# Layer 0's weights moved to the free axis by VectorE transpositions, and paired Strassen products in another order

## The chip, the cores and the metric

The kernel runs on one core of a Trainium2 chip. The metric is the device time of one execution in microseconds (us), taken as the median of repeated runs. A profile of one such execution gives the time of every instruction on the five engines: TensorE (PE, its weight loads PEld), VectorE (DVE), ScalarE (ACT), GpSimd (POOL) and the queue of SyncE (SP), which issues the DMA transfers here.

## The reference

A stack of four graph layers works on 128 graphs of 64 nodes with 512 features, all in float32. Before every layer there is a layer norm and a ReLU, after it the layer's output is added to x. The layer that the first half of the change touches is layer 0:

```python
h = jnp.maximum(_layernorm(x), 0.0)              # (128, 64, 512)
q, k = jnp.split(h @ Wqk, 2, axis=-1)
v = h @ Wv
agg = jnp.einsum('bij,bjd->bid', adj, k * mask[:, :, None])
w = inv_scale * mask * jnp.einsum('bid,bid->bi', q, agg)      # one number per node
x = x + jax.nn.softmax(w, axis=1)[:, :, None] * v             # over the 64 nodes of a graph
```

So each graph has 64 numbers w, one for each node, and a softmax over them. Layer 1 is an attention over the 64 nodes with adj as a factor (`weight = adj * exp(query @ key.T)`, divided by its row sums, times value). Layer 2 is an eight-headed attention with an output projection. Layer 3 mixes three powers of a transition matrix, each with its own weight.

## The kernel before, in words

**Tiles.** The 8192 nodes ("tokens") are cut into 32 blocks of 256 tokens, that is two halves of 128 (`TT = 2`). A half has one token on each of the 128 partitions, so a partition range of 64 is one graph. The normalised block `h` is transposed by TensorE (`transposed`, line 191) to `hT`, and copied out of PSUM by ACT (line 194) for one half and DVE (line 196) for the other.

**The products.** Every multiplication of a 256x512 block by a 512x512 weight is done by seven products of half size (the Winograd form of Strassen's method). The sums of quarters of the weight are formed once (`formed`); the sums of quarters of the block are formed by POOL for each block (`sums`, lines 215 to 218): S1 = A21 + A22, S2 = S1 - A11, S4 = A12 - S2, S3 = A11 - A21. Product 1 needs only `hT`, product 5 needs S1, product 6 needs S2 and product 4 needs only `hT`. A `Product` owns two PSUM banks, `ab` (quarters a and b) and `dc` (quarters d and c). Products 1 and 6 write `ab`, products 5 and 4 write `dc`; these four are the early ones. Then `keep_ab` copies a to `p1` (ACT, line 275) and makes `u2 = b + p1` (DVE, line 276), and `keep_dc` copies c to `p5` (ACT, line 283 or 287). Only then may the late products 2, 7 and 3 add to the same banks. The outputs are put together by `store` or `store_T` (DVE lines 298 to 314, ACT lines 297 and 318, POOL lines 301 and 321).

In the trace the early and the late products of one kind carry the same name: `ab_g`, `dc_g` are those of the first weight of a step ("g"), `ab_v`, `dc_v` those of the second ("v"); `ab_q` and `ab_k` are layer 2's.

**Two products side by side.** `side_by_side` takes one or two parts that share the block. It writes, in program order: `first` of part 1 (products 1 and 6, `keep_ab`), then the work listed in `between[0]`, then `second` of part 1 (products 5 and 4, `keep_dc`), both of part 2, then the late products of part 1 with the work of `between[1]` ahead of them, the late products of part 2 with `between[2]` ahead. Layers 0 and 1 and the q and k of layer 2 go through it with two parts; the output projection of layer 2 with one; layer 3 has its own order.

**Steps.** Layers 0 and 1 run in steps of one block: layer 0 of blocks b and b+1, then layer 1 of b and b+1, and so on through the 32 blocks, so that four steps make a round. The end of a layer-0 step, `layer0_end`, is put off into `between[0]` of the step behind it. There also stands `prepare`, the norm of the block of the step after that (DVE lines 168 to 175, POOL line 173, ACT line 180), and in `between[2]` its transposition. So in the second and the third step of a round DVE and ACT have the put-off softmax of layer 0 and the norm that layer 1 needs from its result.

**Layer 0's softmax.** In `layer0`, w comes out as one number per partition (line 504, a product with a running sum, for each half). The softmax needs all 64 numbers of a graph on the free axis. Line 511 (DVE) spreads w by the identity to `wd` (128 x 2 x 64, a diagonal for each half). In `layer0_end` `graph_sums` (line 392, TensorE) multiplies it by `ones_bd`, which has ones in the blocks of a graph: each partition then has the 64 numbers of its graph in PSUM, named `sm_w` in the trace. Line 522 (DVE) takes the minimum, line 525 subtracts, line 528 (ACT, once for each half) takes the exponential and its sum, line 533 (ACT) the exponential of the own number, lines 535 and 536 (DVE) make the weight, and line 538 (DVE) adds it times v to x.

**Order.** The source gives only data dependencies and a priority by program order. When the program is built, a scheduler writes one fixed list of instructions for each engine from that; on the chip each engine takes its list strictly in order and waits at the head of it.

Of the kernel before, what the change touches and what calls it, by code (L numbers as in the profile page):

```python
# [8 lines left out]
FP = mybir.dt.float32  # L9
AF = mybir.ActivationFunctionType  # L10
ALU = mybir.AluOpType
AX = mybir.AxisListType

P = 128
N = 64
# [3 lines left out]
TT = 2  # L19
# [6 lines left out]
def kernel(ctx: ExitStack, tc: tile.TileContext, a: dict, out: bass.AP):  # L26
# [7 lines left out]
    nc = tc.nc  # L34
# [9 lines left out]
    small = ctx.enter_context(tc.tile_pool(name="small", bufs=3))  # L44
# [8 lines left out]
    def rows(b: int):  # L53
        return slice(b * T, (b + 1) * T)

    def load_x(b: int, source, stage: int):
        x = big.tile([P, TT, D], FP, tag="x", name=f"x{stage}_{b}", bufs=4)
        nc.sync.dma_start(x, tokens(source))
        return x

    def load_adjT(b: int, stage: int):
        adjT = med.tile([P, TT, N], FP, tag="adjT", name=f"adjT{stage}_{b}")
        nc.sync.dma_start(adjT, tokens(adjT_d[rows(b), :]))
        return adjT
# [59 lines left out]
    first = load_x(0, x_d[rows(0), :], 0), load_adjT(0, 0)  # L124
# [16 lines left out]
    eye = const.tile([P, N], FP, tag="eye", name="eye")  # L141
    for g in range(2):
        h = slice(g * N, (g + 1) * N)
# [8 lines left out]
    for i in range(n_bd):  # L152
        e = const.tile([P, TT, P], FP, tag=f"bd{i}", name=f"bd{i}")
# [68 lines left out]
    class Product:  # L222
# [37 lines left out]
        def temp(self, tag):  # L260
            return snap.tile([P, F], FP, tag=tag, name=f"{tag}_{self.name}")

        def first(self, ops, w):
            self.early(ops, w, (1, 6))
            self.keep_ab()

        def second(self, ops, w, bias=None):
            self.early(ops, w, (5, 4))
            self.keep_dc(bias)

        def keep_ab(self):
# [23 lines left out]
        def store(self, y):  # L295

            nc.scalar.copy(y[:, 0, :F], self.a)
            nc.vector.tensor_tensor(self.u3, self.b, self.p1, ALU.add)  # L298
            nc.vector.tensor_tensor(y[:, 1, :F], self.d, self.u3, ALU.add)
            nc.vector.tensor_tensor(y[:, 0, F:], self.c, self.u2, ALU.add)  # L300
            nc.gpsimd.tensor_tensor(y[:, 1, F:], self.u3, self.p5, ALU.add)  # L301
# [37 lines left out]
    def side_by_side(*parts, between=()):  # L339

        between = iter(between)
        made = []
        for ops, w, bias, store, name in parts:
            p = Product(name, bias is not None)
            p.first(ops, w)
            if not made:
                for act in next(between, ()):
                    act()  # L350
            p.second(ops, w, bias)
            made.append(p)
        for p, (ops, w, bias, store, name) in zip(made, parts):
            for act in next(between, ()):
                act()
            p.late(ops, w)
            store(p)
        for acts in between:
            for act in acts:
                act()  # L360
# [16 lines left out]
    def neighbour_sums(ps, e, us):  # L377

        for t in range(TT):
            for g in range(2):
                nc.tensor.matmul(
                    ps[t][half[g ^ t]], e[half[g], t, :], us[t][half[g]], start=True, stop=True
                )
        return [(0, slice(0, P), slice(0, P))] + [(1, half[g], half[1 - g]) for g in range(2)]

    def graph_sums(e, cols: int, name: str):

        ps = ps_sc.tile([P, cols], FP, tag="sc", name=f"sm_{name}")
        nc.tensor.matmul(ps, ones_bd, e, start=True, stop=True)
        return ps
# [83 lines left out]
    def layer0_values(b: int, hT):  # L477
        ops = sums(hT, f"0_{b}")
        gv = big.tile([P, 2, TT, D], FP, tag="qk", name=f"gv_{b}")
        return ops, gv, (ops, w0v, None, lambda p: p.store(gv[:, 1]), f"v0_{b}")  # L480

    def layer0(b: int, x, adjT, hs, hT, between, ready=None):

        ops, gv, *part = ready or layer0_values(b, hT)
        am = small.tile([P, TT, N], FP, tag="am", name=f"am_{b}", bufs=2)
        nc.gpsimd.tensor_tensor(
            am,
            adjT,
            mcol[:, b * TT : (b + 1) * TT].unsqueeze(2).to_broadcast([P, TT, N]),
            ALU.mult,  # L490
        )
        pa = [ps_tr.tile([P, D], FP, tag="tr", name=f"pa_{b}_{t}") for t in range(TT)]
        aggs = [
            med.tile([P, D], FP, tag="agg", name=f"agg_{b}_{t}", bufs=2) for t in range(TT)
        ]
        for t, to, at in neighbour_sums(pa, am, hs):
            nc.scalar.copy(aggs[t][to], pa[t][at])

        side_by_side(
            (ops, m0, None, lambda p: p.store(gv[:, 0]), f"g0_{b}"), *part, between=between  # L500
        )
        w = small.tile([P, TT], FP, tag="w", name=f"w_{b}")
        for t in range(TT):
            nc.vector.scalar_tensor_tensor(
                aggs[t], gv[:, 0, t, :], msc[:, b * TT + t : b * TT + t + 1], aggs[t],
                ALU.mult, ALU.mult, accum_out=w[:, t : t + 1],
            )


        wd = small.tile([P, TT, N], FP, tag="e", name=f"wd_{b}")  # L510
        nc.vector.tensor_tensor(
            wd,
            eye.unsqueeze(1).to_broadcast([P, TT, N]),
            w.unsqueeze(2).to_broadcast([P, TT, N]),
            ALU.mult,
        )
        return x, gv, w, wd

    def layer0_end(b: int, x, gv, w, wd):
        wrow = graph_sums(wd.rearrange("p t i -> p (t i)"), TT * N, f"w_{b}")  # L520
        mn = small.tile([P, TT], FP, tag="mx0", name=f"mn0_{b}")
        nc.vector.tensor_reduce(
            mn, wrow.rearrange("p (t i) -> p t i", t=TT), AX.X, ALU.min
        )
        nc.vector.tensor_tensor(w, w, mn, ALU.subtract)
        tot = small.tile([P, TT], FP, tag="tot", name=f"tot_{b}")
        for t in range(TT):
            nc.scalar.activation(
                wd[:, t, :], wrow[:, t * N : (t + 1) * N], AF.Exp, bias=mn[:, t : t + 1],
                scale=-1.0, accum_out=tot[:, t : t + 1],  # L530
            )
        ex = small.tile([P, TT], FP, tag="ex", name=f"ex_{b}")
        nc.scalar.activation(ex, w, AF.Exp, scale=-1.0)
        att = small.tile([P, TT], FP, tag="att", name=f"att_{b}")
        nc.vector.reciprocal(att, tot)
        nc.vector.tensor_tensor(att, att, ex, ALU.mult)
        for t in range(TT):
            nc.vector.scalar_tensor_tensor(
                x[:, t, :], gv[:, 1, t, :], att[:, t : t + 1], x[:, t, :], ALU.mult, ALU.add
            )  # L540
# [75 lines left out]
    def layer2_in(b: int, hT, between=()):  # L616

        ops = sums(hT, f"2_{b}")
        qk = big.tile([P, 2, K, T], FP, tag="qk", name=f"qk_{b}")
        side_by_side(*(  # L620
            (ops, w, bias, lambda p, i=i, bias=bias: p.store_T(qk[:, i], bias), f"{'qk'[i]}2_{b}")
            for i, (w, bias) in enumerate(zip(made1[5], (b2q, b2k)))
        ), between=between)
        return qk, ops
# [318 lines left out]
    for i, (layer, b) in enumerate(steps):  # L943
        between = [[], [], []]
        for n, end in open_end:
            between[n].append(end)
        if i + 1 < len(steps):
            between[0].append(lambda: prepare(i + 1))
            between[2].append(lambda: turned(i + 1))
        else:  # L950
            between[0].append(lambda: prepare2(0))
            between[2].append(lambda: turned2(0))
        if layer == 0:
            softmax = layer0(b, *loaded[b], *normed[i], between, ready)
            ready = None
            open_end = [(0, lambda b=b, softmax=softmax: layer0_end(b, *softmax))]
        else:
            attention = layer1(b, *loaded[b], *normed[i], between)
            open_end = [
                (1, lambda b=b, a=attention: layer1_end(b, loaded[b][0], *a, x1[b]))  # L960
            ]
        if i == len(steps) - 3:
            setup = setup2()
            made2 = next(setup)
# [15 lines left out]
    qk, ops = layer2_in(0, normed2[0], [[], [end for _, end in open_end]])  # L980
# [6 lines left out]
    for b in range(n_blk):  # L987
        x, adjq = loaded2[b]
# [7 lines left out]
        if b + 1 < n_blk:  # L996
            qk, ops = layer2_in(b + 1, normed2[b + 1])
# [90 lines left out]
```

## Time and profile before

| | |
|---|---|
| median of 3 runs | 2751.52 us (2751.24 to 2751.78) |
| the profiled execution | 2750.76 us, span in the profile 2749.0 us |
| granted TensorE clock | 0.996 of full |
| PE busy | 2696.7 us, 98% of the span |
| DVE, POOL, ACT busy | 1628.3, 1279.6, 895.0 us |
| layers 0 and 1 | from the start to about 1060 us |
| one round of four steps | about 61.7 us (from one line 511 to the next but one) |

A line of the page or of a query gives the start and the duration in us, the engine, the source line, the operation, the tile written and the tile read, and in brackets how long the engine stood idle before it and what released it. A busy PE does not mean a PE at its peak, so what a stage costs is read from the starts of its instructions, not from busy time. The chain of waits follows the last instruction of a window back to what released it.

### The profile page before, as it was taken

Reading aid. Unit: us, or ns where it says so; the run is one execution under the profiler, and the core shown is the slowest. Engines: PE = TensorE matmul, PEld = TensorE weight load, DVE = VectorE, ACT = ScalarE, POOL = GpSimd, SP = SyncE. Lnnn points to the kernel's source line nnn. Section 1 sums busy time; section 2 is a strip of 40 time slices with the busy share of each in tenths; the row PEclk is TensorE's granted clock in tenths of the full one; section 3 lists DMA queues with packets and bytes.
Section 4 is the critical chain, followed back from the end, with each engine's and each line's share of the span. In section 5 each row is a group of like instructions: output and inputs, shape, how many; then the busy total and the mean of one; then the engine's idle time right before and its main releaser. Section 6 shows DMA issues by size and latency. Waiting matters only on the chain.

```text
span 2749.0 us, 53245 instructions
## 1 busy us (share of the span) xinstructions
PE 2696.7 (98%) x21336; PEld 2352.7 (86%) x21336; DVE 1628.3 (59%) x4105; ACT 895.0 (33%) x2132; POOL 1279.6 (47%) x1648
## 2 busy tenths in 40 slices
PE   7899999999999999999999999999989999999999
PEld 5688888888888887899999999999878888888888
DVE  4466666666656667565655655556546555565553
ACT  2233333333333333333333333333322222222221
POOL 2433434343333436555555555554455444444443
PEclk9999999999999999999999999999999999999999
DMA  4111101001111113111111111111111111111110
GB/s 143 40 42 34 49 33 34 34 34 34 44 39 41 41 34 102 38 36 36 53 36 43 46 36 53 36 36 53 48 49 58 57 50 50 50 50 50 50 49 31
DMA packets 102488, 128.53 MB, mean 47 GB/s; under 512 B 40544, under 2 KB 50016, under 8 KB 102240
## 3 DMA queue, kind: packets, MB, share of 16 engines
q1 hardware_dynamic: 100576, 123.02, 13.3%
q8 instruction: 168, 2.75, 0.4%
q10 hardware_dynamic: 1664, 2.10, 0.2%
q14 instruction: 80, 0.66, 0.1%
HBM read 74.76 MB, written 50.33 MB: 46 GB/s over the span
## 4 chain that ended last, share of the span: by engine, by line
PE 87%; DVE 6%; POOL 3%; ACT 2%; DMA 1%; issue 1%; SPq 0%; DVEq 0%; ACTq 0%; POOLq 0%
PE ab_y L250 12%; PE ab_v L250 10%; PE dc_y L250 9%; PE dc_v L250 7%; PE ab_q L243 4%; PE ab_k L243 4%; PE tr L191 4%; PE ab_o L250 4%; PE ab_g L250 4%; PE dc_k L243 3%; PE dc_q L243 3%; PE dc_o L250 3%; PE ab_g L243 3%; PE dc_g L250 2%; PE pz L849 2%; PE dc_g L243 2%
## 5 line engine op out<-in xcount | busy, mean ns | idle before, releaser
L180 ACT ACTIVATE h<-x,nmr,rstd 128x512 f32<-128x512 f32 x256 | 196.5, 807 | 197.8 <-DVE nmr L175 197.6
L173 POOL TENSOR_TENSOR rstd<-ve,neghalf 128x2 f32<-128x2 f32 x128 | 89.4, 699 | 351.3 <-DVE ve L171 351.2
L250 PE MATMUL ab_v<-L_Wv,hT 128*128 128x256 f32 x768 | 200.6, 384 | 2.3 <-DVE u_v L276 1.3
L250 PE MATMUL ab_v<-L_Wv,S 128*128 128x256 f32 x768 | 198.5, 381 | 0.8 <-POOL S L216 0.8
L250 PE MATMUL dc_v<-L_Wv,S 128*128 128x256 f32 x768 | 197.6, 380 | 0.0
L250 PE MATMUL ab_y<-L_Wk,S 128*128 128x256 f32 x768 | 187.3, 380 | 0.0
L168 DVE BATCH_NORM_STATS2 stats<-x 128x6 f32<-128x512 f32 x256 | 165.4, 679 | 27.3 <-DMA x<-x 22.0
L250 PE MATMUL dc_y<-L_Wk,S 128*128 128x256 f32 x768 | 177.9, 381 | 0.0
L194 ACT COPY hT<-tr 128x512 f32<-128x512 f32 x128 | 74.7, 584 | 304.3 <-PE tr L191 280.2
L215 POOL TENSOR_TENSOR S<-hT 128x256 f32<-128x256 f32 x128 | 108.2, 845 | 130.5 <-ACT hT L194 125.0
L250 PEld LDWEIGHTS ab_v<-L_Wv,S 128*128 128x128 f32 x768 | 147.0, 192 | 21.8 <-POOL S L216 1.6
L250 PEld LDWEIGHTS ab_y<-L_Wk,S 128*128 128x128 f32 x768 | 146.5, 191 | 20.1
L250 PEld LDWEIGHTS dc_v<-L_Wv,S 128*128 128x128 f32 x768 | 146.4, 191 | 20.1
L250 PEld LDWEIGHTS dc_y<-L_Wk,S 128*128 128x128 f32 x768 | 143.6, 190 | 18.2
L191 PE MATMUL tr<-ident,h 128*128 128x128 f32 x1024 | 142.5, 280 | 15.5 <-ACT h L180 13.2
L196 DVE COPY hT<-tr 128x512 f32<-128x512 f32 x128 | 87.5, 684 | 110.6 <-PE ab_v L250 106.7
L250 PEld LDWEIGHTS ab_v<-L_Wv,hT 128*128 128x128 f32 x768 | 135.1, 193 | 16.5 <-DVE u_v L276 1.7
L678 POOL TENSOR_TENSOR e<-e,r 128x512 f32<-128x512 f32 x64 | 66.4, 1058 | 163.8 <-DVE r L677 163.8
L191 PEld LDWEIGHTS tr<-ident,h 128*128 128x128 f32 x1024 | 116.2, 142 | 28.9 <-ACT h L180 23.1
L250 PE MATMUL ab_y<-L_Wk,z 128*128 128x256 f32 x512 | 126.3, 379 | 0.0
L787 DVE SCALAR_TENSOR_TENSOR hu<-h,u 128x512 f32<-128x512 f32 x128 | 100.2, 817 | 27.2 <-ACT h L180 27.0
L301 POOL TENSOR_TENSOR gv<-u_g,p_g 128x256 f32<-128x256 f32 x32 | 23.3, 729 | 198.7 <-DVE u_g L298 198.7
(273 smaller groups left out, 6574.8 us busy)
## 6 DMA issues: line engine op xcount, KB each, us to landing
x<-x SPq DMA_DIRECT2D x128, 512.0 KB, 3.4
x<-in_x_dram SPq DMA_DIRECT2D x32, 512.0 KB, 3.6
out_dram<-x SPq DMA_DIRECT2D x31, 512.0 KB, 2.7
adjq<-in_adj_dram SPq DMA_DIRECT2D x64, 64.0 KB, 2.4
L_Wk<-in_L_Wk_dram SPq DMA_DIRECT2D x16, 256.0 KB, 4.2
adjT<-in_adjT_dram SPq DMA_DIRECT2D x32, 64.0 KB, 1.9
L_Wv<-in_L_Wv_dram SPq DMA_DIRECT2D x8, 256.0 KB, 5.3
adj<-in_adj_dram SPq DMA_DIRECT2D x32, 64.0 KB, 2.0
```

What stands on the lines that cost most here:

```text
L168: nc.vector.bn_stats(stats[:, t, :], x[:, t, :])
L173: nc.gpsimd.tensor_tensor(rstd, ve, neghalf, ALU.pow)
L180: nc.scalar.activation(h, x[:, t, :], AF.Relu, bias=nmr[:, t : t + 1], scale=rstd[:, t : t + 1])
L191: nc.tensor.transpose(pt[:, k, :], h[:, k * P : (k + 1) * P], ident)
L194: nc.scalar.copy(ht, pt)
L196: nc.vector.tensor_copy(ht, pt)
L215: nc.gpsimd.tensor_tensor(S1, A21, A22, ALU.add)
L243: nc.tensor.matmul(dst[:, m * P : (m + 1) * P], w[:, place, k, m * P : (m + 1) * P], left[:, k, :], start=key not in self.begun, stop=last ...
L250: nc.tensor.matmul(dst, left[:, k, :], w[:, place, k, :], start=key not in self.begun, stop=last and k == 1, skip_group_check=True,)
L678: nc.gpsimd.tensor_tensor(eh, eh, r.unsqueeze(2).to_broadcast([P, TT * hq, N]), ALU.mult)
L787: nc.vector.scalar_tensor_tensor(hu, hs[t], 1.0, us[s], ALU.mult, ALU.mult, accum_out=sij[:, s, t : t + 1],)
L849: nc.tensor.matmul(pz[t * 2 + g][:, :, c, :], hs[t][h, c * P : (c + 1) * P], tt[h, t], start=True, stop=True,)
```

## The change

Two edits. In layer 0 the diagonal (line 511) and the product with `ones_bd` (line 392) go; in their place w is broadcast along the free axis and transposed by DVE in blocks of 32 x 32, once for the own 32 partitions and once for the other 32 of the graph, to a tile in SBUF from which the minimum and the exponentials are then taken. And wherever two parts stand side by side, the early products run 1, 5, 6, 4, where they ran 1, 6, 5, 4; `keep_ab` then comes after products 6 and 4, behind the work of `between[0]`.

```diff
-        def first(self, ops, w):
-            self.early(ops, w, (1, 6))
-            self.keep_ab()
-
-        def second(self, ops, w, bias=None):
-            self.early(ops, w, (5, 4))
+        def first(self, ops, w, beside: bool = False):
+
+            self.early(ops, w, (1, 5) if beside else (1, 6))
+            if not beside:
+                self.keep_ab()
+
+        def second(self, ops, w, bias=None, beside: bool = False):
+            self.early(ops, w, (6, 4) if beside else (5, 4))
+            if beside:
+                self.keep_ab()
             self.keep_dc(bias)
...
             p = Product(name, bias is not None)
-            p.first(ops, w)
+            p.first(ops, w, len(parts) > 1)
             if not made:
                 for act in next(between, ()):
                     act()
-            p.second(ops, w, bias)
+            p.second(ops, w, bias, len(parts) > 1)
             made.append(p)
...
-        wd = small.tile([P, TT, N], FP, tag="e", name=f"wd_{b}")
-        nc.vector.tensor_tensor(
-            wd,
-            eye.unsqueeze(1).to_broadcast([P, TT, N]),
-            w.unsqueeze(2).to_broadcast([P, TT, N]),
-            ALU.mult,
-        )
-        return x, gv, w, wd
-
-    def layer0_end(b: int, x, gv, w, wd):
-        wrow = graph_sums(wd.rearrange("p t i -> p (t i)"), TT * N, f"w_{b}")
+        wrow = small.tile([P, TT, 2, 32], FP, tag="e", name=f"wrow_{b}")
+        wide = w.unsqueeze(2).to_broadcast([P, TT, 32])
+        nc.vector.transpose(wrow[:, :, 0], wide)
+        for q in range(4):
+            own, other = (slice(i * 32, (i + 1) * 32) for i in (q, q ^ 1))
+            nc.vector.transpose(wrow[own, :, 1], wide[other])
+        return x, gv, w, wrow.rearrange("p t h i -> p t (h i)")
+
+    def layer0_end(b: int, x, gv, w, wrow):
         mn = small.tile([P, TT], FP, tag="mx0", name=f"mn0_{b}")
-        nc.vector.tensor_reduce(
-            mn, wrow.rearrange("p (t i) -> p t i", t=TT), AX.X, ALU.min
-        )
+        nc.vector.tensor_reduce(mn, wrow, AX.X, ALU.min)
         nc.vector.tensor_tensor(w, w, mn, ALU.subtract)
         tot = small.tile([P, TT], FP, tag="tot", name=f"tot_{b}")
         for t in range(TT):
             nc.scalar.activation(
-                wd[:, t, :], wrow[:, t * N : (t + 1) * N], AF.Exp, bias=mn[:, t : t + 1],
+                wrow[:, t], wrow[:, t], AF.Exp, bias=mn[:, t : t + 1],
                 scale=-1.0, accum_out=tot[:, t : t + 1],
             )
```

## The prediction

> **What bounds the kernel now.** I read the page's busy times first, then the stretch of layers 0 and 1 (rounds of four steps, 300 to 1040 us), then its waits, then the chain of waits through one round.
>
> ```profile
> PE 2696.7 (98%) x21336; PEld 2352.7 (86%) x21336; DVE 1628.3 (59%) x4105; ACT 895.0 (33%) x2132; POOL 1279.6 (47%) x1648
> ```
>
> ```profile
> 300.00:1040.00 740.00, 732.95 (x5132) 612.30 (x5132) 481.51 (x1297) 279.96 (x719) 284.68 (x362) 1.00 0.12 40
> ```
>
> The second line is the table by stretch: PE, PEld, DVE, ACT and POOL busy, then clock and DMA. PE looks like the bound (99%), DVE has 65%. The waits of the same stretch (total us, times, longest) show what the change aims at:
>
> ```profile
> PEld ab_g L243 <- POOL S L216: 5.8, 12, 0.9
> PEld sm_w L392 <- DVE wd L511: 3.8, 12, 0.3
> DVE mn L522 <- PE sm_w L392: 14.2, 11, 1.4
> PEld tr L191 <- ACT h L180: 7.7, 26, 0.3
> ```
>
> The first is product 6 waiting for S2 in a round's third step (layer 1 of the first block). The last says that in that step PE also waits for the norm. The chain of waits through the second and third step shows how much that decides:
>
> ```profile
> 527.79 0.23 PE sm_w L392 x2
> ...
> 529.58 1.42 DVE x L538 x2
> ...
> 534.60 0.80 ACT h L180
> 535.39 0.26 ACT p_v L283
> 535.65 0.28 ACT gv L297
> ...
> 535.95 0.43 DVE u_g L298
> ...
> 544.59 0.75 DVE x L538
> ```
>
> From line 392 at 527.8 to the second x at 544.6 no PE work stands in the chain. Two links follow and are the same in both kernels: from x in the second step to the end of that block's h, 5.82 us (529.58 to 535.40); from x in the third step to the late `ab_v`, 6.71 us (544.59 to 551.30). From 551.57 to the next round's w the chain is PE alone. So a round is set by PE in its steps four and one and by a DVE-ACT chain in two and three. What PE saves in those two is lost unless that chain gets shorter.
>
> **What the change takes from PE.** `sm_w` costs PE a slot of 0.215 us where nothing waits: the product before starts loading at 526.55, the second one after at 528.50, 1.95 us, less two products of 0.865. In the third step it costs 0.5 us (540.40 to 541.90, less 0.89 and a lead of 0.1). The S2 wait costs 0.63 us there (538.88 to 540.40, less 0.89). With order 1, 5, 6, 4 product 5 comes between, which needs S1 (ready at 538.08), and S2 (540.35) is then in time. The four early products of g and v need 4 x 0.89 + 4 x 0.866 = 7.02 us in place of 8.16. All this lies under the chain in the third step; only 0.215 us could count in the second. I book nothing.
>
> **What it puts on the chain.** I compared the instruction orders of both kernels as built. Two things differ beside the exchange:
>
> ```
> after, DVE, third step:  transposes, hc_1, mn, be, w-mn, recip, att, x, x, BNStats x2, aggr, u_g (line 280), ...
> after, PE:               late ab_g waits for DVE (that u_g); it stood ahead of w-mn and x before
> after, ACT, second step: exp of half 0, copy agg_1 x2, exp of half 1, ex, ... h, h, p_v (a), p_v (c), gv
> ```
>
> `keep_ab` is now behind `between[0]` in program order, so u_g of the g part stands behind the x update and the statistics, and the late `ab_g` is released at x + 3.05 us (x pair 1.33, statistics 1.20, aggregate 0.1, u_g 0.42).
>
> *Price of a transpose.* The trace has none. Nearest is a one-source SBUF copy of 64 float32 on 64 partitions, twice, on different partitions:
>
> ```profile
> 12.85 0.39 DVE L145 COPY eye<-ident 64x64 f32<-64x64 f32 x2
> 549.22 0.24 DVE L169 BATCH_NORM_AGGREGATE mv<-stats 128x2 f32<-128x6 f32 x2
> ```
>
> The copies take 0.186 each and 0.39 for both: no overlap. The aggregates take 0.165 each but 0.24 for both: short instructions can overlap by 0.09. Which holds for the transposes?[...] By the aggregates' overlap five would cost about 5 x 0.1 = 0.5 us;[...] here the TensorE side costs 0.215 in the stream[...], and there are five transposes, not one. The copy's 0.186[...] is the lower end;[...] I take 0.25, nearer the copy.
>
> *Second step, from w to x.* Before 4.8 us (wd at 524.81, x at 529.58; 4.83 in nearly every round, 4.17 in two of them). After: transposes 5 x 0.25, u_v 0.42, gv 0.34 and 0.42 (they stand between), mn 0.29, handoffs 0.06 = 2.8; ACT then exp 0.30, the two agg copies 1.16, exp 0.30, and from ex to x 0.61 (528.97 to 529.58). Sum 5.15: **+0.35**. The product leaves the chain (line 522 waited 1.4 us for it), and transposes and agg copies come in.
>
> *Second step, from h to DVE's u_g.* Before, p_v (a) stood ahead of h on ACT; now it comes after. One more copy at the chain's pitch: **+0.25** (p_v to gv, 535.39 to 535.65).
>
> *Third step, from u_g to x.* DVE is busy end to end here, so each instruction counts: wd's slot 0.38 out, first transpose 0.2 in, four more 4 x 0.25 in, lost overlap 0.1, be (0.14) now behind mn. u_g out ahead of w-mn saves nothing, since `att` waited 0.37 us for ACT there. **+0.8.**
>
> Sum 1.4 us a round; 15 rounds in the steady order (the first is mixed with setup, +-3 us): 21, and 2 x 0.6 for the two rounds that start from 4.17: 22.
>
> *Layer 2.* Products 1, 5, 6, 4 wait for nothing new on POOL. But in the built order u_k now stands behind `x + b1v` (line 928), which waits for the x transfer:
>
> ```profile
> 1518.01 1.29 DVE L928 TENSOR_TENSOR x<-x,L_bv 128x512 f32<-128x512 f32 x2 [2.26 <-DMA x<-x]
> 1519.02 0.97 PEld L243 LDWEIGHTS ab_k<-hT,L_Wk 128*128 128x128 f32 x8
> ```
>
> u_k would end 1.7 us after line 928 starts (1.20 + 0.42 + handoff); the late `ab_k` wants to start 1.01 after it in this block. Over the blocks that distance is mostly 2.3 to 3.0 us, and below 1.7 in six, short by 0.02 to 0.7: **+2**. At the start of layer 2 one 3.8 us wait of `ab_q` for S2 shortens by one product, -0.9. Layer 3 has its own code. SP's list is unchanged, and POOL only moves some norms' rstd behind sums of S.
>
> Sum: +22 + 2 - 0.9 = +23 on the profiled 2750.76 us, which stands 0.8 below the median: 2774 against 2751.52. With the copy's 0.186 each round loses 0.8 us, sum +14 (2765)[...].
>
> **The rivals.** *PE's savings count after all (faster).* PE's work in the third step is 7.02 + 2.67 + 0.91 = 10.6 us, where it takes 12.42 (538.88 to 551.30); with the 0.215 that makes 2.0 us a round, 30 in all. For: the waits above exist. Against: the chain would have to shrink by 2 us; even transposes at no cost leave it 0.7 (ACT's agg copies bound the second step) + 0.4 - 0.25 = about 0.9 shorter. It decides where a transpose costs under some 0.12 us: then -5 to -14, say 2742.
>
> *No change.* At about 0.12 us each, +0.25 on ACT against the rest gives zero a round: 2752.
>
> *Layer 2's u_k decides as well.* A transfer that lands 1 us later puts u_k behind the late `ab_k` in most of the 30 blocks, at about 0.7 each: +20 more, 2793. For: line 928 waits for a DMA in 29 blocks. Against: the distances above are mostly over 2 us, and nothing moves that load.
>
> *The change does not do what it says.* The built order has 32 products fewer and the stated order of 1, 5, 6, 4; I leave this out.
>
> **How the numbers follow.** Forecast (slower, 2765 to 2784 by the price) 0.70; layer 2 on top 0.12; no change 0.08; faster 0.10. A difference of 0.2% (5.5 us) is about what a measurement can tell from none. The range goes from 2753 (a transpose at 0.12) to 2795: some 0.14 lies below, 0.04 above. Faster 0.10, same 0.08, slower 0.82.
>
> **What would show it.** Right: no `sm_w`, no wait of PE for S2 in the third step; in its place PE's late `ab_g` (line 250 for layer 0, 243 for layer 1) waits for DVE's u_g (line 280), about 2.5 to 3 us in the third step and 0.4 in the second; the distance between the two x of a round grows from 15.0 us to about 16, a round from 61.7 to 63.1; the transposes at 0.25; layer 2 and 3 within 3 us of before. Wrong: transposes near 0.1 us with overlap, or u_g not late; then the round shrinks. If the rounds keep 61.7 and layer 2 grows, the third rival holds.

## The result and the profile after

The change makes the kernel slower: 2785.89 us (median of four runs, 2784.55 to 2787.58) against 2751.38 beside it, a ratio of 1.0127 with an interval of 1.0111 to 1.0142. The forecast was 2774, in a range of 2753 to 2795. The profiled execution of the changed kernel took 2787.58 us and its span 2785.8, 36.8 more than before.

The busy times of the page, and below them the table by stretch for the steady rounds of layers 0 and 1 (PE, PEld, DVE, ACT, POOL busy, then granted clock, DMA share, GB/s):

```profile
PE 2709.8 (97%) x21272; PEld 2364.7 (85%) x21272; DVE 1634.9 (59%) x4233; ACT 892.0 (32%) x2132; POOL 1277.6 (46%) x1648
```

```profile
300.00:1040.00 740.00, 707.03 (x4894) 593.25 (x4893) 476.88 (x1331) 270.75 (x688) 269.59 (x346) 0.97 0.11 36
```

PE has 64 records fewer and yet more busy time. In the steady rounds it went from 99% busy to 96%, and the mean granted clock from 1.00 to 0.97. Both numbers point at the same place. The waits of PE in that stretch (us in total, times, longest):

```profile
PE ab_g L243 <- DVE u_g L280: 30.0, 12, 2.5
PE ab_g L250 <- DVE u_g L280: 3.0, 11, 0.3
```

The waits for S2 and for `sm_w`'s diagonal are gone. In their place the late `ab_g` waits for DVE's u_g, 2.5 us in every third step and 0.3 in every second, as the prediction said. The chain of waits through the same two steps of a round as before:

```profile
541.41 1.42 DVE x L538 x2
...
546.43 0.80 ACT h L180
547.23 0.26 ACT p_v L279
547.49 0.27 ACT p_v L287
547.76 0.28 ACT gv L301
...
548.07 0.44 DVE u_g L302
...
557.33 1.42 DVE x L538 x2
```

From x to x it is 15.92 us where it was 15.01, and the `p_v` of line 279 right behind h, at 547.23, is the ACT copy that the prediction put there. The transpositions of the third step, in the time-ordered list of DVE's instructions:

```profile
553.14 0.23 DVE L516 STREAM_TRANSPOSE wrow<-w 128x64 f32<-128x64 f32 x1
554.11 0.98 DVE L519 STREAM_TRANSPOSE wrow<-w 32x64 f32<-32x64 f32 x4
```

Four take 0.98 us, 0.245 each and end to end; the prediction's 0.25 was an estimate, set above the copy's 0.186.

**Where the round grew.** The starts of the four x updates in DVE's list cut a round into four stretches. Over the 14 rounds from the second on each keeps its value within some 0.1 us, except where two values stand, and except the very last of them (11.9 and 11.8 us in the last column, ahead of the last round):

| kernel | second step's x to third step's x | to layer 1's first x | to its second | to the next second step's x | time, us |
|---|---|---|---|---|---|
| before | 15.02 | 19.05 | 16.68 | 10.95 | 2751.4 |
| after | 15.92 | 20.57 in 13 rounds, 19.05 in one | 16.68 | 11.56 | 2785.9 |

A round went from 61.70 to 64.73 us. Half of the 3.03 was forecast: 0.90 and 0.61 in the first and last column. The other half, 1.52 in the second column, was not. The trace shows it behind the wait, in PE's list of a usual round and in the table by stretch:

```profile
560.38 2.08 PE L243 MATMUL ab_g<-hT,fold 128*128 128x128 f32 x8 [2.50 <-DVE u_g L280]
562.25 1.70 PE L243 MATMUL ab_g<-S,fold 128*128 128x128 f32 x8
```

```profile
558.00:560.00 2.00, 0.00 (x0) 0.00 (x0) 2.00 (x6) 0.37 (x1) 0.00 (x0) 1.00 0.00 0
560.00:562.00 2.00, 1.62 (x7) 1.62 (x8) 1.52 (x8) 0.00 (x0) 0.70 (x1) 0.54 0.00 0
562.00:564.00 2.00, 2.00 (x13) 2.00 (x12) 1.30 (x5) 1.52 (x2) 0.00 (x0) 0.60 0.00 0
```

Before 560.38 PE does nothing for 2.5 us, and then it is granted 0.54 and 0.60 of its clock for two stretches of 2 us. From the late product 2 to the start of product 3 it takes 3.41 us (560.38 to 563.79) in place of 1.88. The one round that keeps 19.05 us has the same wait, and its products at full rate (the clock is 1.00 from 496 to 502 us):

```profile
497.19 1.16 PE L243 MATMUL ab_g<-hT,fold 128*128 128x128 f32 x8 [2.50 <-DVE u_g L280]
498.18 1.06 PE L243 MATMUL ab_g<-S,fold 128*128 128x128 f32 x8
```

So the theory after the result, called A in the expectations: the chain of DVE and ACT grew by about 1.5 us a round, and the long wait on PE costs nothing by itself but lowers the clock behind it, for another 1.5. The rivals: B, the transpositions are the whole cost; C, the slow products are not due to the idle PE or are not on the path; D, filling the idle stretch only moves the loss to the drains behind it.

### The profile page after: what moved, and what is told of

It reads as the page before. It is cut to its first block, busy times and chain, and to the rows that moved or that the text cites. A ratio compares the mean times of both kernels' runs of the same rounds, so it can differ in the third digit from the quotient of the medians.

```text
span 2785.8 us, 53188 instructions
## 1 busy us (share of the span) xinstructions
PE 2709.8 (97%) x21272; PEld 2364.7 (85%) x21272; DVE 1634.9 (59%) x4233; ACT 892.0 (32%) x2132; POOL 1277.6 (46%) x1648
## 4 chain that ended last, share of the span: by engine, by line
PE 83%; DVE 10%; ACT 2%; DMA 2%; POOL 2%; issue 2%; SPq 0%; DVEq 0%; ACTq 0%; POOLq 0%
PE ab_y L250 12%; PE ab_v L250 9%; PE dc_y L250 9%; PE dc_v L250 6%; PE ab_g L243 4%; PE ab_k L243 4%; PE ab_o L250 4%; PE ab_q L243 4%; PE tr L191 4%; PE dc_k L243 3%; PE dc_o L250 3%; PE dc_q L243 3%; PE dc_g L243 2%; PE pz L849 2%; PE ab_g L250 2%; DVE x L538 2%
## 5 line engine op out<-in xcount | busy, mean ns | idle before, releaser
L243 PEld LDWEIGHTS ab_g<-hT,fold 128*128 128x128 f32 x512 | 68.4, 204 | 61.9 <-DVE u_g L280 47.3
L243 PE MATMUL ab_g<-hT,fold 128*128 128x128 f32 x512 | 78.5, 300 | 40.5 <-DVE u_g L280 40.5
```

The source lines that it names most:

```text
L243: nc.tensor.matmul(dst[:, m * P : (m + 1) * P], w[:, place, k, m * P : (m + 1) * P], left[:, k, :], start=key not in self.begun, stop=last ...
```

## Experiments

### The two parts alone, and the late keep_ab alone

The transpositions alone: `first`, `second` and `side_by_side` as before.

```diff
-            self.early(ops, w, (1, 5) if beside else (1, 6))
-            if not beside:
-                self.keep_ab()
+            self.early(ops, w, (1, 6))
+            self.keep_ab()
...
-            self.early(ops, w, (6, 4) if beside else (5, 4))
-            if beside:
-                self.keep_ab()
+            self.early(ops, w, (5, 4))
```

> The five transpositions alone: the paired products keep the order 1, 6, 5, 4 with keep_ab between them, as before the change. Theory A (longer DVE chain, plus a TensorE clock that falls after the 2.5 us in which the late ab_g product waits for DVE's late u_g): the late wait is gone, because u_g stands ahead of the weights and of layer 0's end on DVE again; no stretch of the third step shows a granted clock below 0.9; from w to x in the second step stays about 5.4 us (+0.6), the third step loses up to 0.9. Round +0.6 to +1.5, time 2758 to 2775 us. Theory B (the transpositions and their exponentials are the whole cost): time as with the full change, 2780 to 2790 us.

The order alone: the diagonal `wd` and the product `sm_w` of the kernel before, with the changed `first` and `second`.

```diff
-        nc.vector.transpose(wrow[:, :, 0], wide)
-        for q in range(4):
-            own, other = (slice(i * 32, (i + 1) * 32) for i in (q, q ^ 1))
-            nc.vector.transpose(wrow[own, :, 1], wide[other])
...
+    def layer0_end(b: int, x, gv, w, wd):
+        wrow = graph_sums(wd.rearrange("p t i -> p (t i)"), TT * N, f"w_{b}")
```

> The order 1, 5, 6, 4 with the late keep_ab alone; the diagonal and the product with ones stay as before. Theory A: the third step has the late wait for u_g again (1.5 to 2.5 us of PE), and with it a granted clock near 0.55 in the 3 to 4 us behind it, so that most of the 1.5 us a round not foreseen is here: round +1 to +2.5, time 2766 to 2785 us. Theory B (transpositions alone): within 5 us of the time before, about 2752 us.

The changed kernel with `keep_ab` ahead of what lies between:

```diff
-            self.early(ops, w, (1, 5) if beside else (1, 6))
-            if not beside:
-                self.keep_ab()
+            self.early(ops, w, (1, 5, 6) if beside else (1, 6))
+            self.keep_ab()
...
-            self.early(ops, w, (6, 4) if beside else (5, 4))
-            if beside:
-                self.keep_ab()
+            self.early(ops, w, (4,) if beside else (5, 4))
```

> The changed kernel with its paired products as 1, 5, 6, then keep_ab, then what lies between, then 4 and keep_dc: only the place of keep_ab (and of product 6) differs from the changed kernel. Theory A: the wait of the late ab_g product for u_g falls from 2.5 us to under 0.5, the clock stays at 1.0, and 1.5 to 2.2 us a round come back: 2752 to 2766 us. Theory B: at most the wait itself was hidden, time stays at 2780 to 2788 us.

| kernel | x to x | to layer 1's x | to its second | to the next x | time, us | ratio to before |
|---|---|---|---|---|---|---|
| transpositions alone | 15.71 | 19.05 | 16.68 | 11.55 | 2763.84 | 1.0041 (1.0026 to 1.0055) |
| order alone | 15.02 | 19.05 | 16.68 | 10.95 | 2748.38 | 0.9992 (0.9986 to 0.9999) |
| early keep_ab | 16.25 | 20.4 | 16.68 | 11.55 | 2787.84 | 1.0131 (1.0115 to 1.0146) |

The transpositions cost 1.29 us a round and no clock (1.00 from 300 to 1040 us), 13 us in all: B is out, since the full change costs 35. The order alone costs nothing and brings nothing: PE's wait for S2 is gone, and every stretch is that of before. There A missed: I had expected the long wait to come with the late u_g. PE's list tells why it does not:

```profile
356.45 0.49 PE L396 MATMUL sm_w<-wd,ones_bd 128*128 128x128 f32 x2 [0.65 <-DVE wd L515]
...
362.41 1.16 PE L243 MATMUL ab_g<-hT,fold 128*128 128x128 f32 x8 [0.23 <-DVE u_g L280]
```

The release is at x + 3.05 (x at 359.36), as forecast. But PE has already waited 0.65 for the diagonal and done `sm_w`, and x comes 0.9 us earlier in the round; so PE arrives only 0.23 before the release, at x + 2.82. In the changed kernel it arrives at x + 0.56.

The third run is the most instructive miss. With `keep_ab` early, u_g is no longer late, and the time is that of the full change. PE's list in its third step:

```profile
369.64 1.97 PE L191 MATMUL tr<-ident,h 128*128 128x128 f32 x8 [2.64 <-ACT h L180]
371.40 1.83 PE L250 MATMUL ab_v<-L_Wv,hT 128*128 128x256 f32 x4
```

PE runs on through the late `ab_g` and then waits 2.64 us for h, the end of the same chain, and the clock falls there (0.50 from 370.03 to 372.03 us). So the place of `keep_ab` is not the cause. PE was made quicker than the chain by 2.5 us in this step, and the wait stands wherever the first thing that needs the chain stands. With the transpositions alone a surplus of 2.2 us comes in two pieces, 0.68 us for S2 and 1.49 for h:

```profile
353.11 1.16 PE L243 MATMUL ab_g<-S,fold 128*128 128x128 f32 x8 [0.68 <-POOL S L216]
...
363.67 1.36 PE L191 MATMUL tr<-ident,h 128*128 128x128 f32 x8 [1.49 <-ACT h L180]
```

and the clock stays at 1.00.

### Is it the idle PE that costs the clock?

Filling the wait with products that nobody reads:

```diff
+            if name[:3] == "g1_" and int(name[3:]) % 2 == 0:
+                fill = ps_sc.tile([P, P], FP, tag="sc", name=f"fill_{name}")
+                for _ in range(12):
+                    nc.tensor.matmul(fill, ident, ident, start=True, stop=True)
             p.late(ops, w)
```

> The changed kernel, with twelve 128x128 products of the unit matrix with itself put on PE just ahead of the late ab_g product of the third step; what they write is read by nobody. They fill about 2.6 us in which PE would only wait for u_g; the wait, DVE's order and the place of u_g stay as they are. Theory A (idle PE, clock falls, next products slow): the clock behind the wait stays near 1.0, ab_g products 2 and 7 take 2.0 us again in place of 3.6, and the round loses 1.2 to 1.6 us: 2762 to 2770 us. Theory C (the products behind the wait are slow for another reason, or their slowness is not on the path): 2784 to 2790 us, with the products still at 3.6 us or the round no shorter.

It took 2812.46 us, 1.022 of before (1.0205 to 1.0236): slower still. Behind the filled wait the clock did stay at 1.00 (from 367.33 to 377.33 us), and the late products 2, 7 and 3 took 1.14, 1.06 and 1.06 us. But the stretch to layer 1's x was 21.67 us, and 22.65 in six rounds of 14. The scheduler, which orders DVE by its own estimate of when things are ready, had seen PE busy longer and moved DVE's drain of the late `ab_g`. DVE's list in the changed kernel (x at 364.65) and in this one (x at 367.33), and PE's in this one:

```profile
370.54 0.41 DVE L309 TENSOR_TENSOR u_g<-ab_g,p_g 128x256 f32<-128x256 f32 x1
```

```profile
376.52 0.42 DVE L309 TENSOR_TENSOR u_g<-ab_g,p_g 128x256 f32<-128x256 f32 x1
```

```profile
378.92 1.06 PE L377 MATMUL sc<-hT,gT 128*64 128x64 f32 x24 [0.93 <-DVE gT L318]
```

That drain runs at x + 9.19 where it ran at x + 5.89, and the scores (`sc`) wait for it. In the six rounds of 22.65 us another 0.98 us is lost. The mean granted clock from 300 to 1040 us is 0.99, where the changed kernel has 0.97 and the kernel before 1.00, so it still falls in that stretch; in which stage is not shown. The run shows that the fill kept the clock at the place where it stood, but not what that is worth, since it changed two things at once. So the order had to be tied. In the next two kernels, edges that set only the issue order hold DVE, ACT and POOL to the changed kernel's sequence, and the fill is the only difference: in both traces these three engines run the same list of instructions as in the changed kernel's, from the first to the last. It stands in the third steps of the 14 rounds from the second on; ten and four products:

```diff
+    def behind(later, earlier):
+        if later in rec and earlier in rec:
+            tc.add_manual_dep(
+                rec[later].ins, rec[earlier].ins.name,
+                mybir.DependencyInfo(mybir.DependencyClass.NoSync, mybir.DependencyReason.DATA),
+                reason="issue order of the changed kernel",
+            )
...
+    for b in range(2, n_blk - 2, 2):
+        kept_order(b)
...
+                for _ in range(10):
+                    nc.tensor.matmul(fill, ident, ident, start=True, stop=True)
```

> The changed kernel with ten 128x128 products of the unit matrix with itself (read by nobody) just ahead of the late ab_g product of the third step, in 14 of the 16 rounds, and with the issue order of DVE, ACT and POOL tied to that of the changed kernel, so that only PE's idle stretch is filled. Theory A (2.5 us of idle PE lowers the TensorE clock, and only that costs): granted clock 1.0 behind the wait, the stretch from the third step's x to the next x falls from 20.57 to 19.05 us in each of these rounds, 14 x 1.5 = 21 us come back: 2762 to 2768 us. Theory D (filling PE merely moves the loss to the drains behind it, as in the fill before): the stretch stays above 20 us, 2780 us or more.

> The same with four products in place of ten, about 0.9 us of the 2.5, so that about 1.6 us of idle PE are left, as long as the 1.49 us with which the transpositions alone kept the clock. Theory A with the length of the gap as its measure: the clock stays at 1.0 and the time equals that of the full fill, 2762 to 2768 us. If any wait of over a microsecond were enough to lower the clock, or if the drop hung on where the wait stands: 2780 to 2788 us, with a clock near 0.55 behind the wait.

They took 2766.90 us (1.0062, 1.0047 to 1.0077) and 2766.98 us (1.0056, 1.0039 to 1.0073), and in both every round has 15.92, 19.05, 16.68 and 11.55 us. The whole 1.52 us a round is back, the clock behind the wait is 1.00 (361.54 to 366.54 us in the first, 362.30 to 367.30 in the second), and four products are enough. PE's list of the second, with 1.61 us of idleness left:

```profile
359.40 1.05 PE L373 MATMUL fill_g<-ident 128*128 128x128 f32 x8
362.06 1.16 PE L253 MATMUL ab_g<-hT,fold 128*128 128x128 f32 x8 [1.61 <-DVE u_g L290]
363.05 1.06 PE L253 MATMUL ab_g<-S,fold 128*128 128x128 f32 x8
```

C and D fall. The late `ab_g` starts at x + 3.06 here and in the changed kernel alike: no wait became shorter on the path, PE was only kept from being idle.

### Is the chain from w to x on the path in the second step?

Before the change, `sm_w` stood behind product 6. It needs only the diagonal, and can go ahead of product 1:

```diff
         for t, to, at in neighbour_sums(pa, am, hs):
             nc.scalar.copy(aggs[t][to], pa[t][at])
+        for act in ahead:
+            act()
...
+    def layer0_sums(b: int, wd, rows):
+        rows.append(graph_sums(wd.rearrange("p t i -> p (t i)"), TT * N, f"w_{b}"))
...
+            ahead = [lambda b=b, s=softmax: layer0_sums(b, *s[-2:])] if b % 2 == 0 else []
```

> The kernel before, with the product with ones of layer 0's first block issued in the second step directly behind the neighbour sums, ahead of product 1, in place of behind product 6; nothing else. Theory A (the round is set in the second and third step by DVE's and ACT's chain from w to x, not by PE): from w to x in the second step falls by about 1.2 us and the round by 0.5 to 1.2, until PE sets it again: 2735 to 2745 us. Rival (PE or the chain behind x sets these steps): within 3 us of the time before.

> The kernel before with the product with ones moved as in the run beside it, and the paired products as 1, 5, 6, keep_ab, 4, keep_dc. Theory A: with the chain shorter, PE sets the steps, and the new order, which takes away PE's wait for S of 0.3 to 0.6 us a round, counts for the first time: 3 to 9 us below the run beside it. Rival: the same time as the run beside it within 2 us, or above it where the later product 4 delays a drain.

The first took 2746.27 us (0.9983, 0.9976 to 0.9990), a gain, though a little less than the least expected; the second 2749.70 (0.9999, 0.9990 to 1.0007), a miss. In both the stretch to the second step's x fell from 10.95 to 10.25 us: the chain is on the path there, and shortening it is worth 0.70, what the prediction gave as the most. But x to x grew, to 15.32 (15.67 in two rounds) and 15.72 in most rounds, so that nearly half or all of it was given back. In the second kernel the cause is the one predicted for the change: with the order 1, 5, 6, 4 both `p_v` copies stand behind h on ACT. For the first I suspected DVE's u_g, put by the scheduler between the two halves of x, and tied it behind ve:

```diff
+    for b in range(0, n_blk, 2):
+        behind(("u2", f"g0_{b + 1}"), ("ve", f"1_{b}"))
+        behind(("h", f"1_{b}", 0), ("p1", f"v0_{b + 1}"))
```

> The kernel before with the product with ones moved ahead in the second step, as in the run that took 2746 us, and with DVE's u_g of that step (the drain of ab_g, L276) tied behind ve, into the 0.8 us in which DVE waits for POOL's rstd; there the scheduler had put it between the two halves of x. Theory A (every DVE instruction between w and h in the second step is on the path): x to x falls from 15.32 to between 14.95 and 15.05 us, the round by another 0.3, 14 rounds by 4: 2740 to 2744 us. Rival (PE or another queue has become the limit in that step): 2745 to 2748 us.

2744.35 us (0.9977, 0.9968 to 0.9986), but x to x stayed at 15.32: the rival was right. ACT's list shows the new limit:

```profile
348.75 0.37 ACT L306 COPY gv<-ab_g 128x256 f32<-128x256 f32 x1 [0.27 <-PE ab_g L259]
```

The link in the chain behind h now waits for PE's late `ab_g`: with the chain 0.7 us shorter, PE sets this step. This kernel and the one without the tie lie within each other's spread; both beat the kernel before by about 0.2%, and are the fastest here.

### Why the second step grew by 0.61

In the changed kernel, ACT's list of a second step (x of layer 0 at 348.73):

```profile
344.44 0.59 ACT L501 COPY agg<-pa 128x512 f32<-128x512 f32 x1 [1.51 <-PE pa L388]
346.15 0.35 ACT L528 ACTIVATE wrow<-wrow,mn 128x64 f32<-128x64 f32 x1 [1.12 <-DVE mn L524]
...
346.60 1.17 ACT L501 COPY agg<-pa 64x512 f32<-64x512 f32 x2
347.79 0.35 ACT L528 ACTIVATE wrow<-wrow,mn 128x64 f32<-128x64 f32 x1
```

ACT, which takes its list in order, waits 1.12 us for mn, with two copies behind the waiting exponential that are ready, and then does these copies, 1.17 us, ahead of the second exponential. I tied the exponentials behind the copies, once with the transpositions alone and once in the changed kernel:

```diff
+    for b in range(0, n_blk, 2):
+        for c in rec["agg", b + 1]:
+            for t in range(TT + 1):
+                tc.add_manual_dep(
+                    rec["exp", b, t].ins, c.ins.name,
+                    mybir.DependencyInfo(mybir.DependencyClass.NoSync, mybir.DependencyReason.DATA),
+                    reason="issue order",
+                )
```

> The transpositions alone (order 1, 6, 5, 4, as in the run that took 2764 us), with ACT's order in the second step tied: the three copies of the neighbour sums (agg from pa) ahead of layer 0's exponentials, as in the kernel before, where the scheduler had put the first exponential between the first and the second copy. Theory A (the +0.6 us from w to x in the second step are not the transpositions' time but ACT: it waits 1.1 us for mn with 1.17 us of ready copies behind the waiting exponential): the stretch from layer 1's x to layer 0's x falls from 11.55 to about 10.25 us, the round by 1.3, 14 rounds by 18: 2744 to 2749 us, no longer slower than before. Rival (the transpositions themselves lengthen it): the stretch stays above 11.3 us, 2760 us or more.

> The changed kernel with the same tie of ACT's order and nothing else. Theory A: the same 1.3 us a round come back in the second step; the wait for the late u_g in the third step, the drop of the clock behind it and the 0.9 us from x to x stay: 2765 to 2770 us. Rival (the stretches are not independent, the gain is eaten by a longer wait in the third step): above 2775 us.

```profile
335.35 1.77 ACT L499 COPY agg<-pa 128x512 f32<-128x512 f32 x3 [1.51 <-PE pa L386]
337.13 0.35 ACT L526 ACTIVATE wrow<-wrow,mn 128x64 f32<-128x64 f32 x1
```

| kernel | x to x | to layer 1's x | to its second | to the next x | time, us | ratio to before |
|---|---|---|---|---|---|---|
| transpositions alone, tied | 16.18 | 19.05 | 16.68 | 10.32 | 2753.77 | 1.0012 (1.0005 to 1.0019) |
| changed kernel, tied | 16.18 | 20.57 in 6, 19.05 in 8 | 16.68 | 10.32 | 2763.49 | 1.0046 (1.0031 to 1.0062) |

The stretch falls by 1.23 us in both, to 0.63 below the kernel before: in the second step the transpositions are a gain, and the 0.61 was ACT's order. The first run still missed its range, by 5 us, because x to x grew by 0.47. In the trace that is one instruction: the first `agg` product of DVE in the third step, 0.74 us with the transpositions alone, is 1.21 here.

```profile
350.59 0.74 DVE L504 SCALAR_TENSOR_TENSOR agg<-gv,msc,agg 128x512 f32<-128x512 f32 x1
```

```profile
346.65 1.21 DVE L506 SCALAR_TENSOR_TENSOR agg<-gv,msc,agg 128x512 f32<-128x512 f32 x1
```

In POOL's list a sum of S (0.73 us) begins 0.07 before it here, and 0.61 before it in the faster case, where it is all but over. In the tied changed kernel the sum begins 0.26 before, `agg` takes 1.01, and the stretch is longer by 0.26. The three cases go together: from 0.26 to 0.07 us the sum has 0.19 more left to run when `agg` begins, and `agg` takes 0.20 longer. That POOL's sum is the cause is not shown: no run took POOL away.

The second run came out 1.5 us under its range: the wait for u_g was 2.13 us there and not 2.50, and the stretch to layer 1's x was 20.57 us in 6 rounds of 14 only, nearly every other one, with the same instructions and the same wait. In one of the six the granted clock is 0.66 over the 3 us from the end of the wait (423.40 to 426.40 us), in the round ahead of it 1.00 (361.17 to 364.17).

The changed kernel's trace shows what decides there. In it, as in that of the kernel before, the granted clock takes the values 1.00 and 0.50 and changes only at instants that stand a whole number of 3.41 us apart, and in the steady rounds each fall lasts one such step (560.18 to 563.59 us behind the wait shown first). Two pairs of neighbouring steps in the changed kernel, the upper from the round ahead of the one that keeps 19.05 us, the lower from that round (stretch, PE busy, ..., then the clock, third from the end):

```profile
430.48:433.89 3.41, 1.45 (x13) 1.45 (x14) 2.97 (x9) 0.00 (x0) 0.69 (x1) 1.00 0.00 0
433.89:437.30 3.41, 3.41 (x19) 3.41 (x18) 3.03 (x11) 2.15 (x4) 1.12 (x2) 0.50 0.02 5
```

```profile
495.33:498.74 3.41, 1.55 (x14) 1.56 (x14) 2.92 (x10) 0.00 (x0) 0.70 (x1) 1.00 0.00 0
498.74:502.16 3.42, 3.42 (x27) 3.17 (x26) 3.42 (x13) 2.74 (x5) 1.46 (x2) 1.00 0.01 2
```

In both rounds the wait is 2.50 us. In the upper one 1.97 us of idle PE lie within one step, and the clock halves in the next; in the lower one the wait begins 0.64 us ahead of a step's start, 1.86 us of idle PE are left within the step, and the clock stays. Over the 14 rounds of the changed kernel it fell behind each of the 13 steps with 1.97 to 2.50 us of idle PE, and not behind the one with 1.86. So in this kernel where the wait of 2.50 us falls among the steps decides, and not its length; that 2.13 us lowered the clock in 6 rounds of the tied kernel and not in the other 8 fits this, but where those waits lie among the steps is not shown. Idle time alone does not tell every fall: in the changed kernel's setup the clock is 0.50 from 78.90 to 89.14 us, and in the step ahead of it (75.49 to 78.90) PE was busy all the time. What counts there stays open.

## Why the prediction was right, and what it missed

The sign, the mechanism and the size of the chain held. Its terms, for one round:

| step of the prediction | forecast | measured |
|---|---|---|
| a transposition | 0.25 us | 0.245 |
| PE's savings (`sm_w`, S2) | nothing | S2: nothing (order alone, 61.70 before and after); `sm_w` was not removed by itself, but with both gone and the clock kept (the tied fill) a round is 63.2 |
| w to x, second step | +0.35 | +0.61 (11.56 less 10.95) |
| x to u_g, second step | +0.25 | +0.28 (6.65 less 6.37) |
| u_g to x, third step | +0.80 | +0.62 (9.27 less 8.65) |
| release of the late `ab_g` | x + 3.05 | x + 3.06 |
| behind the third step's x | nothing | +1.52 in 13 of 14 rounds |

*Second step.* The order on ACT with the copies between the exponentials was foreseen, and also that mn would come 2.8 us after w (2.86). The term was mis-sized in the exponential: taken as 0.30, from before, where its source lay in PSUM (0.31 us each in the mean, with the source in SBUF 0.34); the first now has a pitch of 0.45 to the copy behind it (346.15 to 346.60), its own 0.35 and the reading of its sum, and the second 0.34 (347.79 to 348.13 in ACT's list). The 2 x 0.6 for the two rounds that start from 4.17 was not there: their stretch before the change is 10.95 us like the others', with w later in it.

*Third step.* From u_v to x it grew by 0.77 (4.53 less 3.76), the 0.8 of the forecast; ahead of it the first `agg` took 0.74 in place of 0.88, which I had not booked. The forecast counted the transpositions end to end (5 x 0.25) and without overlap into the instruction behind them (lost overlap 0.1): an assumption, which no trace of before shows for a transposition. The four of 32 partitions run so here: they take 0.98 us, and `hc` behind them begins 0.03 us after their end (555.12 against 555.09 in DVE's list), where the second `gv` begins 0.08 ahead of the end of the first (553.66 against 553.74). Behind the one of 128 partitions `gv` begins 0.05 ahead of its end (553.32 against 553.37). By the aggregates' overlap the five would have taken about 0.5 us, and they take 1.2.

*The step that failed* is "all this lies under the chain". It asked only whether PE's savings shorten the round, and not what an idle PE does next. The wait of "2.5 to 3 us" was in the text as a sign to look for, at no cost. As a wait it has none: 19.05 us behind it, with 0, 1.5, 1.6 or 2.5 us. What it costs is the clock, 13 x 1.52 = 20 us. The traces show what it takes: a wait of 2.50 us lowered the clock in 13 of 14 rounds (the changed kernel), 2.13 in 6 of 14 (tied on ACT), 1.61 in none (four products); in the changed kernel by whether 1.97 us or more of it lay within one step of 3.41. Without these falls the change costs about 16 us, as it does with the fill, not 34.

*The rest.* The total came closer than its terms, because two errors met. The first x of layer 0 that ends a second step came 4.9 us earlier than before (159.42 to 154.54), where "+-3" stood; with the transpositions alone it is 6.0, with the order alone none, so it comes with them. The 14 rounds behind it added 40.3 in place of 22, what follows them (the rest of the last round, layers 2 and 3) 1.4 in place of 1.1: 40.3 - 4.9 + 1.4 = 36.8, the difference of the two spans. That the result lies inside the range is in part luck too: the forecast by the price of a transposition ended at 2784, with a dear end that no trace shows, and the upper end of 2795 was drawn for layer 2's u_k, which had no part in it.

*The rivals.* "PE's savings count" is out by the order alone and, for both savings together, by the tied fill. "Layer 2's u_k" is out: that wait is 0.3 us once in the whole program.

## What to carry to other kernels

When work is taken from an engine that is not on the path, ask where its idle time will then stand, and whether it will be one piece: here waits of 0.68 us for S2 and of 0.65 for `sm_w`'s diagonal left the clock at 1.00, and one wait of 2.5 us cost 1.52 us a round, as much as the change's whole chain (1.51). When a part of the input of an engine comes earlier, look at what the scheduler puts in front of it in the engine's list (ACT waited 1.12 us here with ready copies behind); one tie of ACT's order took the changed kernel from 2786 to 2763 us, in part by the shorter chain and in part by fewer falls of the clock. And before an added instruction is taken as a probe, see that it left the other engines' order alone.

## What the hardware showed unasked

In the changed kernel's steady rounds the granted clock halved for 3.41 us, on a beat of 3.41 us, behind each of 13 steps in which PE stood idle for 1.97 to 2.50 us, and not behind the one with 1.86. A wait of 2.50 us did it in 13 rounds of 14, one of 2.13 (tied on ACT) in 6 of 14, and one of 1.61 (four products) in none; the prediction had booked 2.5 to 3 us at no cost. Four products of 128x128 in the wait of 2.50 us, 1.05 us of work, prevented it. The first `agg` of 128x512 on DVE took 0.74, 1.01 or 1.21 us where a sum of S on POOL had begun 0.61, 0.26 or 0.07 us ahead of it; that the sum is the cause is not shown.
